# Second layer of a relational graph network: slot sums in three banks, placings three octets late, closes an octet later

## The chip, the cores and the metric

The kernel runs on one core of a Trainium2 chip. The metric is device time in microseconds for one execution. Five engines have programs of their own: PE (TensorE), DVE (VectorE), ACT (ScalarE), POOL (GpSimd) and SP (SyncE). They tell each other by semaphores what is done.

## The reference, cut to what matters

```python
def _rgcn_conv(x, src, dst, et, basis, comp, root, bias):
    W = jnp.einsum('rb,bio->rio', comp, basis)
    xw = jnp.einsum('ni,rio->nro', x, W)
    msgs = xw[src, et]
    seg = dst * N_REL + et
    summed = jax.ops.segment_sum(msgs, seg, num_segments=N_NODES * N_REL)
    cnt = jax.ops.segment_sum(jnp.ones((msgs.shape[0],), x.dtype), seg, num_segments=N_NODES * N_REL)
    mean = summed / jnp.maximum(cnt, 1.0)[:, None]
    agg = mean.reshape(N_NODES, N_REL, HIDDEN).sum(axis=1)
    return agg + x @ root + bias
...
h = x
for l in range(N_LAYERS):
    h_new = _rgcn_conv(h, src, dst, edge_type, basis[l], comp[l], root[l], bias[l])
    h_new = jax.nn.relu(h_new)
    h = h_new + h
...
x = _layernorm(x + h)
```

There are 12500 nodes, 200000 edges sorted by destination, 8 relations, 8 bases, 2 layers and 128 features, all in float32. The last line stands for the layernorm over the features of `x` plus the network's output.

## The kernel before

**Tiles and stages.** The edges are cut into 1563 tiles of 128, and 8 tiles make an octet, 196 octets in a layer (`NQ`). The nodes are cut into 98 blocks of 128 (`NT`). A layer goes through the octets in order. The first layer takes roughly the first 2320 us. It sums edges by node and relation, applies the relations' weights, and on the way stores the second layer's table `y_d` in memory: for each node and relation the message that an edge of that kind carries. The second layer, which the change concerns, gathers rows of `y_d` and sums them by destination.

**One octet of the second layer.** `FULL` = 192 of the 196 octets go this way (the last four go another, `add_rows`):

- POOL: `gather` issues eight indirect gathers (L677), each 128 rows of 512 bytes into a tile of `rows`. `rows` is a ring of seven octets. The gathers of octet n + 7 write the buffer of octet n, and so wait for the slot sum of n. From octet 190 on (`NQ - LATE`) gathers also wait for the last sum written by then, three octets back (`("done", 1)`).
- DVE: `slot_hots` makes eight matrices of 128x32 (L1090) that say for each edge of a tile which of 32 slots its destination has, times the edge's weight (one over the count), and, in the same step, the placing one-hot of 128x256 (L1093) that says for each slot where its node stands. It runs two octets ahead of the sums.
- PE: `slot_sums` (L1441), 8 matmuls, recorded as 16 instructions, sums the rows into the slots. Its output is one fixed PSUM bank, `misc`, the fourth quarter of `po1`.
- ACT: the copy (L627) takes the slots from that bank into a buffer `ys`, a ring of four.
- PE: `place_sums` (L1466), for the octet before, adds the copied slots to the accumulator of their block, `s0` or `s1` in turn. The first placing of a block (it *opens* the block) also adds the root term (L1470), from a copy of the block's old rows that ACT made (`open_block`, a ring of three: `id_k`, `id_r`, `jmp`).
- DVE: after a block's last placing `finish` closes it, in two steps. The first adds the carry from the block before (L1298) and takes out the next carry (L1302). The second, an octet later, is relu plus the old rows into `wide` (L1322).

A block takes the placings of two octets. After every eight blocks `norm` transposes `wide` on PE in two halves (L1573, also into `po1`) and DVE adds each half to `x` (L1581), one step of the list `todo` for each octet.

**What sets the order.** Each engine's program is written out by hand, in the order of the calls in the loop over `q` at the end of `ordered_path`. The class `Plan` derives the semaphore waits from what each step reads and writes: from named cells, of which every bank and every ring buffer is one. An engine signals where the program has a `plan.mark`. The gathers' order on POOL is set by `gathers(1, q)`, five octets ahead of the sums.

The output of a slot sum and the copy's ring, in code:

```python
b, bc = misc
m0 = b[:, 3, :]
...
o, oc = ys[q] = ys_r.take()
copy(o, m0, [bc], [oc])
```

## Time and profile before

| | us |
|---|---|
| median of three runs | 4590.76 (4581.87 to 4591.37) |
| profiled execution | 4590.46 |
| its span in the profile | 4588.4 |
| POOL busy, layer 2's gathers | 1475.1 |
| POOL idle just before them | 742.6 |
| PE busy on slot sums | 206.3 |
| DVE busy on slot one-hots | 352.8 |
| ACT busy on copies of the sums | 53.2 |

The span is the time between the first and the last event that the profiler recorded; 2.06 us of the execution lie around it. Busy times by engine and stretch follow, from the view of windows. The columns are the stretch in us, its length, then for each engine busy time and instructions, the mean granted TensorE clock, the DMA engines' busy share and GB/s. The first row is layer 1, the third nearly all of layer 2, the last its end.

```profile
0.00:2320.00 2320.00, 1424.22 (x7835) 1188.03 (x7836) 795.78 (x2491) 381.88 (x821) 1477.14 (x1571) 0.79 0.25 72
2320.00:2450.00 130.00, 31.73 (x178) 20.71 (x177) 20.38 (x66) 8.67 (x20) 70.90 (x77) 0.61 0.21 61
2450.00:4490.00 2040.00, 448.65 (x3492) 276.45 (x3490) 525.36 (x2178) 70.64 (x280) 1354.00 (x1435) 0.52 0.19 52
4490.00:4589.00 99.00, 36.87 (x250) 26.97 (x250) 43.38 (x156) 5.13 (x20) 51.30 (x55) 0.64 0.18 50
```

In the rows of groups and of the timeline that come later, `out<-in` are the program's names with the buffer numbers left out: `po` is the bank of the slot sums, `ys` the copied slots, `sT` the slot one-hots (they live in an old buffer of that name), `pl` and `iota_f` the placing one-hots, `s` a block's accumulator. What stands in brackets is the engine's idle time just before, and what ended it; "remote" means that the trace shows no local event that did. A row of waits has the line that waited, what released it, the total in us, the number of waits and the longest.

### The profile page before, as it was taken

What the parts mean: (1) busy time and instruction counts of PE and PEld (TensorE: products, weight loads), DVE (VectorE), ACT (ScalarE), POOL (GpSimd) and SP (SyncE); (2) the same over time, 40 slices, a digit from 0 to 9 for tenths busy, and PEclk for the clock granted to TensorE, in tenths of its full rate; (3) what the DMA queues carried; (4) which work ended last, traced back from release to release, by engine and by line L of the source; (5) the groups of instructions that cost most, each with busy time, mean ns of one, the idle gap of its engine ahead of it and who ended that gap; (6) DMA issues with size and microseconds to landing.
All of it is one profiled execution on the core that took longest, in us unless ns stands there. A gap on an engine that the chain in (4) does not pass through costs nothing.

```text
span 4588.4 us, 33820 instructions
## 1 busy us (share of the span) xinstructions
PE 1941.5 (42%) x11751; PEld 1512.2 (33%) x11751; DVE 1384.9 (30%) x4891; ACT 466.3 (10%) x1141; POOL 2953.3 (64%) x3135
## 2 busy tenths in 40 slices
PE   2666756666566666656731122222222222222213
PEld 1555555555455555545521111111111111111112
DVE  2544333333333323233321222222222222222224
ACT  0111112121111111111210000000000000000000
POOL 5666666666666666666556666666666666666665
PEclk9878778787777777777865555555555555555556
DMA  3111122232222222222221111212212212122121
GB/s 100 45 50 46 46 62 87 87 92 92 88 69 73 74 69 74 64 66 70 78 71 45 47 51 52 56 46 57 55 47 55 56 47 56 46 56 55 47 55 50
DMA packets 129812, 284.69 MB, mean 62 GB/s; under 512 B 54019, under 2 KB 61773, under 8 KB 129637
## 3 DMA queue, kind: packets, MB, share of 16 engines
q0 software_dynamic: 100064, 205.13, 17.2%
q10 hardware_dynamic: 16971, 52.05, 3.0%
q1 hardware_dynamic: 12602, 25.31, 1.6%
q8 instruction: 94, 1.54, 0.1%
q14 instruction: 81, 0.66, 0.0%
HBM read 223.63 MB, written 58.65 MB: 62 GB/s over the span
## 4 chain that ended last, share of the span: by engine, by line
another core or an unknown queue 64%; PE 20%; issue 8%; ACT 5%; DVE 2%; DMA 0%; POOL 0%; SPq 0%; ACTq 0%; POOLq 0%; DVEq 0%
PE y L1246 7%; PE s L1214 5%; ACT sT L627 2%; PE pt L1345 2%; PE po L1441 2%; ACT ys L627 1%; PE po L1277 1%; DVE dm L1121 1%; ACT y_row L627 1%; PE ct L1345 1%; PE ct L870 0%; PE po L1279 0%; PE ct L871 0%; PE pt L1183 0%
## 5 line engine op out<-in xcount | busy, mean ns | idle before, releaser
L677 POOL DMA_INDIRECT rows<-in_x_dram,idx x1563 | 1476.1, 944 | 841.7 <-issue 440.2
L677 POOL DMA_INDIRECT rows<-y_d,idy x1563 | 1475.1, 944 | 742.6 <-issue 453.3
L1441 PE MATMUL po<-rows,sT 128*32 128x128 f32 x3072 | 206.3, 411 | 1571.3 <-ACT ys L627 1151.2
L1246 PE MATMUL y<-w_sb,sT 128*128 128x128 f32 x3136 | 542.3, 345 | 526.2 <-ACT ys L627 198.6
L1246 PEld LDWEIGHTS y<-w_sb,sT 128*128 128x128 f32 x3136 | 509.4, 254 | 551.6 <-ACT ys L627 207.6
L1121 DVE TENSOR_SCALAR dm<-cols,kr,w 128x128 f32<-128x128 f16 x1563 | 526.2, 403 | 494.2 <-remote 203.1
L1441 PEld LDWEIGHTS po<-rows,sT 128*32 128x32 f32 x3072 | 121.9, 155 | 1658.1 <-ACT ys L627 1190.5
L1090 DVE TENSOR_SCALAR sT<-cols,kr,w 128x32 f32<-128x32 f16 x1536 | 352.8, 303 | 762.9 <-remote 617.7
L1214 PEld LDWEIGHTS s<-dm,rows 128*128 128x128 f32 x3126 | 436.3, 217 | 161.0 <-ACT sT L627 86.5
L1214 PE MATMUL s<-dm,rows 128*128 128x128 f32 x3126 | 450.5, 302 | 64.9 <-ACT sT L627 40.8
L627 ACT ACTIVATE sT<-s 128x512 f32<-128x512 f32 x391 | 212.5, 596 | 783.0 <-remote 556.8
L627 ACT ACTIVATE ys<-po 128x128 f32<-128x128 f32 x192 | 53.2, 277 | 2087.1 <-remote 1936.5
L1298 DVE TENSOR_TENSOR s<-s,carry 128x128 f32<-128x128 f32 x97 | 28.9, 298 | 670.8 <-remote 455.7
L1298 DVE TENSOR_TENSOR po<-po,carry 128x128 f32<-128x128 f32 x98 | 29.2, 298 | 655.1 <-remote 454.7
L1345 PE MATMUL pt<-w_sb,arena 128*128 128x512 f32 x258 | 157.3, 682 | 62.4 <-issue 50.0
L1466 PE MATMUL s<-pl,ys 128*128 128x256 f32 x288 | 167.9, 684 | 0.0
L1277 PE MATMUL po<-pl,ys 128*128 128x256 f32 x392 | 139.4, 440 | 24.2 <-issue 15.8
L627 ACT ACTIVATE y_row<-pt 128x512 f32<-128x512 f32 x131 | 78.4, 598 | 682.0 <-remote 484.2
L870 PE MATMUL ct<-arena,id_h 128*128 128x512 f16 (+1 forms) x188 | 75.5, 421 | 84.4 <-DVE arena L860 37.1
L860 DVE TENSOR_TENSOR arena<-cols,arena 128x129 f16<-128x129 f16 (+62 forms) x188 | 73.6, 408 | 69.5 <-remote 65.5
L1129 DVE TENSOR_SCALAR pl<-cols,pos 128x256 f32<-128x256 f16 x196 | 93.1, 476 | 0.0
L1466 PEld LDWEIGHTS s<-pl,ys 128*128 128x128 f32 x288 | 69.7, 301 | 53.3 <-issue 53.3
(212 smaller groups left out, 1409.7 us busy)
## 6 DMA issues: line engine op xcount, KB each, us to landing
y_d<-y_row ACTq DMA_DIRECT2D x96, 512.0 KB
rows<-in_x_dram,idx POOLq DMA_INDIRECT x1563
rows<-y_d,idy POOLq DMA_INDIRECT x1563
x_g<-in_x_dram SPq DMA_DIRECT2D x24, 512.0 KB
out_dram<-x_g SPq DMA_DIRECT2D x12, 512.0 KB
arena<-in_L_gnn_basis_dram SPq DMA_DIRECT2D x2, 512.0 KB
w_d<-y_row SPq DMA_DIRECT2D x2, 512.0 KB
w_sb<-w_d SPq DMA_DIRECT2D x2, 512.0 KB
```

Source lines behind the costliest of these rows:

```text
L627: act(lambda: nc.scalar.activation(out_t, in_t, AF.Copy), reads, writes)
L677: ins.append(nc.gpsimd.indirect_dma_start(out=t[:, i - q * Q, :], out_offset=None, in_=table_t, in_offset=bass.IndirectOffsetOnAxis(ap=ids ...
L870: nc.tensor.matmul(ct[:, :nb, :], id_h, eq[:, s - s0, :nb, main], start=(s == 1), stop=False)
L1090: vec(in_turn([lambda i=i: nc.vector.tensor_scalar(t[:, i, :], cols[:, :2 * K], kr[:, i0 + i:i0 + i + 1], w[:, i0 + i:i0 + i + 1], op0=ALU ...
L1121: emits.append(lambda i=i: nc.vector.tensor_scalar(t[:, i - q * Q, :wide], cols[:, :wide], ids[:, i:i + 1], w[:, i:i + 1], op0=ALU.is_equa ...
L1129: emits.append(lambda: nc.vector.tensor_scalar(o[:m], cols[:m], pos[:m, g // (2 * R), g % (2 * R):g % (2 * R) + 1], None, op0=ALU.is_equal))
L1214: last = nc.tensor.matmul(s_b[i // 4][0][:, i % 4, :], t[:, i, :], d[:, i, :], start=True, stop=True)
L1246: last = nc.tensor.matmul(y[:m], t[:, r, :nt, :].rearrange("p t k -> p (t k)"), w_sb[:, 0, r, :], start=(r == 0), stop=(r == R - 1))
L1277: ins = nc.tensor.matmul(a, o[:m], t[:m], start=opens, stop=last and not root_in)
L1345: pe(lambda: nc.tensor.matmul(hb[:n].rearrange("p r d -> p (r d)"), hT[:, j * P:j * P + n], w_sb[:, 1, k * H:(k + 1) * H, :].rearrange("p ...
L1441: last = nc.tensor.matmul(m0[i // 2 * 2 * K:(i // 2 + 1) * 2 * K, :], d[:, i, :], t[:, i, :], start=i % 2 == 0, stop=i % 2 == 1)
L1466: ins = nc.tensor.matmul(a, o[:m], t[:m], start=opens, stop=last and not root_in and not fixed)
```

## The change

All of it concerns layer 2; the instructions of layer 1 and POOL's order stay as they are.

- The slot sums use three banks in turn, the first quarters of `y`, `pt` and `ct`, which layer 1 used (`sum_b`).
- The copied slots go to a ring of six (`ys2_r`, in the old buffer `sT1`) in place of four.
- A placing comes three octets after its sum (`LAG`), not one.
- The placing one-hot has a step of its own, `slot_place`, an octet before it is used.
- A block's close starts one octet after its last placing, not in the same.
- The ring of blocks' old rows has four buffers, and each waits only for its own former user (`id_k`, `id_r`, `jmp` waited for all three).
- The norm's two halves use `po0` and `po1`, and each half's add is written one step after its transposes.
- At `q == FULL` the three placings that are left, and their closes, are written one after another.

Code lines move by 10 to 13: in the changed kernel the sums are L1451, placings L1478 and L1482, copies L628, placing one-hots L1097, closes L1307, L1311 and L1331.

```diff
+    LAG = 3
...
-        o, oc = pl[q] = pl2_r.take()
...
-            t[:, i, :], cols[:, :2 * K], kr[:, i0 + i:i0 + i + 1], w[:, i0 + i:i0 + i + 1], op0=ALU.is_equal,
-            op1=ALU.mult) for i in range(Q)]
-            + [lambda: nc.vector.tensor_scalar(o, cols, pos[:, q // (2 * R), q % (2 * R):q % (2 * R) + 1], None,
-                                               op0=ALU.is_equal)]),
-            ["cols", "rel", ("wt", q * Q // P), "pos"], new(c) + new(oc))
-        plan.mark("DVE")
+            op1=ALU.mult) for i in range(Q)]),
+            ["cols", "rel", ("wt", q * Q // P)], new(c))
+
+    def slot_place(q):
+        o, oc = pl[q] = pl2_r.take()
+        vec(lambda: nc.vector.tensor_scalar(o, cols, pos[:, q // (2 * R), q % (2 * R):q % (2 * R) + 1], None,
+                                            op0=ALU.is_equal),
+            ["cols", "pos"], new(oc))
 
     def onehot(l, q, g=None):
 
+        if l == 1:
+            for p in range(q - LAG, FULL if q == FULL + 1 else q - LAG + 1):
+                if 0 <= p < FULL and p not in pl:
+                    slot_place(p)
+            plan.mark("DVE")
         if l == 1 and q < FULL:
             slot_hots(q)
+            plan.mark("DVE")
...
-    old.update({("hb", i): ["id_k", "id_r", "jmp"] for i in range(3)})
+    old.update({("hb", i): [c] for i, c in enumerate(("id_k", "id_r", "jmp"))})
+    hb_b.append(home("sT1", P, "hb", 3))
+    ys2_r = Ring(None, [home("sT1", D, "ys2", i)[0] for i in range(6)], None, None, "ys2")
+    sum_b = [(b[:, 0, :], c) for b, c in (y_full, pt_b, ct_b)]
...
-        t, c = hb_b[k % 3]
+        t, c = hb_b[k % 4]
...
-        b, bc = misc
-        m0 = b[:, 3, :]
+        m0, bc = sum_b[q % 3]
...
-        o, oc = ys[q] = ys_r.take()
-        copy(o, m0, [bc], [oc])
+        o, oc = ys[q] = ys2_r.take()
+        copy(o, m0, [bc], new(oc))
...
-        for h, m in halves:
-            todo.append(lambda h=h, m=m: (turn(h, m), add(h, m)))
-        todo.extend([stats, aggr, root_of] + [lambda: None] * 5 + [one_by, scale, store])
+        todo.append(lambda: turn(*halves[0]))
+        todo.append(lambda: ([turn(*h) for h in halves[1:]], add(*halves[0])))
+        todo.append(lambda: ([add(*h) for h in halves[1:]], stats()))
+        todo.extend([aggr, root_of] + [lambda: None] * 5 + [one_by, scale, store])
...
+    def opening(p):
+        if 2 <= p < NQ and sup(p) != sup(p - 1):
+            open_block(sup(p))
+
+    def closed(j):
+        if j >= 0 and opened_by(j)[1]:
+            a, b = finish(1, sup(j))
+            a()
+            plan.mark("DVE")
+            ending.append((sup(j), b))
+
+    def ended():
+        for j, step in ending:
+            step()
+            plan.mark("DVE")
+            n = j // S
+            if j >= 0 and j % S == S - 1:
+                norm(n)
...
+        ending.clear()
...
-        late = q - 1
+        late = q - LAG
         if q < FULL:
             slot_sums(q)
-        if 0 <= late < FULL:
-            place_sums(late, sup(late), *opened_by(late))
+            if late >= 0:
+                place_sums(late, sup(late), *opened_by(late))
+        if q == FULL:
+            closed(late - 1)
+            for p in range(late, FULL):
+                place_sums(p, sup(p), *opened_by(p))
+                closed(p)
+                ended()
...
-        if sup(q + 2) != sup(q + 1) and q + 2 < NQ:
-            open_block(sup(q + 2))
+        if q < FULL - 1:
+            opening(late + 2)
+        elif q >= FULL:
+            opening(q + 2)
...
-                for j in [late] * (0 <= late < FULL) + [q] * (q >= FULL):
-                    if opened_by(j)[1]:
-                        a, b = finish(1, sup(j))
-                        a()
-                        ending.append((sup(j), b))
+                closed(q if near_end else late - 1)
```

How the instructions stand on the two engines that the change reorders follows, from the middle of layer 2. The first is PE before: sums into `po1`, from the ring `rows0` to `rows6`, with a placing of the octet before after each. Waits on `s_gq` are for gathers, on `s_DVE` for one-hots or closes, on `s_ACT` for copies.

```order
L1441 MATMUL po1_139<-rows2_106,sT0_112 32x128 [waits s_gq2,s_DVE,s_ACT]
L1441 MATMUL po1_139<-rows2_106,sT0_112 32x128 x7
L1466 MATMUL s1_136<-pl0_114,ys0_117 128x256
L1441 MATMUL po1_139<-rows3_107,sT0_112 32x128 [waits s_gq3,s_DVE,s_ACT]
L1441 MATMUL po1_139<-rows3_107,sT0_112 32x128 x7
L1466 MATMUL s0_135<-pl1_115,ys1_118 128x256 [waits s_DVE]
L1470 MATMUL s0_135<-id_r_124,w_sb_75 128x128
```

Now the same place in the changed kernel, with the copied sums in `sT1`:

```order
L1451 MATMUL pt_140<-rows5_109,sT0_112 32x128 [waits s_gq1,s_DVE,s_ACT]
L1451 MATMUL pt_140<-rows5_109,sT0_112 32x128 x7
L1478 MATMUL s0_135<-pl1_115,sT1_113 128x256 [waits s_DVE,s_ACT]
L1482 MATMUL s0_135<-jmp_81,w_sb_75 128x128
L1451 MATMUL ct_141<-rows6_110,sT0_112 32x128 [waits s_gq2]
L1451 MATMUL ct_141<-rows6_110,sT0_112 32x128 x7
L1478 MATMUL s0_135<-pl2_116,sT1_113 128x256
L1451 MATMUL y_137<-rows0_104,sT0_112 32x128 [waits s_gq3,s_DVE,s_ACT]
```

Every sum waited for ACT, that is for the copy just before it. Now every second one does, and the sum between them waits for its gathers alone. The banks differ from sum to sum, and a placing follows a sum that is three octets younger.

The second place is DVE before, two octets with a close (L1298, L1302, L1322):

```order
L1298 TENSOR_TENSOR s1_136<-s1_136,carry1_122 128x128 [waits s_PE]
L1302 TENSOR_SCALAR carry0_121<-s1_136,bias_t_76 128x128
L1090 TENSOR_SCALAR sT0_112<-cols_134,kr_71,w_72 128x32 x8
L1093 TENSOR_SCALAR pl0_114<-cols_134,pos_74 128x256
L1322 SCALAR_TENSOR_TENSOR wide1_131<-s1_136,id_r_124 128x128 [waits s_DVE]
L1090 TENSOR_SCALAR sT0_112<-cols_134,kr_71,w_72 128x32 [waits s_PE]
```

And in the changed kernel:

```order
L1097 TENSOR_SCALAR pl1_115<-cols_134,pos_74 128x256 [waits s_PE]
L1090 TENSOR_SCALAR sT0_112<-cols_134,kr_71,w_72 128x32 [waits s_PE]
L1090 TENSOR_SCALAR sT0_112<-cols_134,kr_71,w_72 128x32 x7
L1307 TENSOR_TENSOR s0_135<-s0_135,carry0_121 128x128 [waits s_PE]
L1311 TENSOR_SCALAR carry1_122<-s0_135,bias_t_76 128x128
L1097 TENSOR_SCALAR pl2_116<-cols_134,pos_74 128x256
L1090 TENSOR_SCALAR sT0_112<-cols_134,kr_71,w_72 128x32 [waits s_PE]
L1090 TENSOR_SCALAR sT0_112<-cols_134,kr_71,w_72 128x32 x7
L1331 SCALAR_TENSOR_TENSOR wide0_130<-s0_135,jmp_81 128x128 [waits s_DVE]
```

The number of instructions is the same. The placing one-hot now stands ahead of the slot one-hots and takes a wait on PE of its own in every second octet, and the slot one-hots between the close's two steps wait for PE too, which they did not before.

More of the change, by code (lines that the diff above doesn't have):

```diff
@@ L1453, in place_sums @@
         o, oc = ys.pop(q)
+        if opens:
+            acc[k] = acc_b[k % 2]
         a, ac = acc[k]
@@ L1566, in norm @@
         halves = [(h, min(4, k - 4 * h)) for h in range(-(-k // 4))]
-        b, bc = misc
         def turn(h, m):
+            b, bc = po_b[h]
             def emit():
@@ L1579, in add @@
         def add(h, m):
+            b, bc = po_b[h]
             zh = z[:, 4 * h:4 * h + m, :]
@@ L1849, in ordered_path @@
         opens, last = opened_by(q)
-        if opens:
+        if opens and q >= FULL:
             acc[k] = acc_b[k % 2]
@@ L1882, in ordered_path @@
         for i in range(2):
-            for j, step in ending:
-                step()
-                plan.mark("DVE")
-                n = j // S
-                if j >= 0 and j % S == S - 1:
-                    norm(n)
-                    if n + 2 < NX:
-                        todo.extend([lambda: None] * 2 + [lambda n=n: load_x(n + 2)])
-            ending.clear()
+            ended()
             if q == NQ - 2:
@@ L1897, in ordered_path @@
             elif i == 0:
-                for j in [late] * (0 <= late < FULL) + [q] * (q >= FULL):
-                    if opened_by(j)[1]:
-                        a, b = finish(1, sup(j))
-                        a()
-                        ending.append((sup(j), b))
+                closed(q if near_end else late - 1)
             if not near_end:
                 break
+        if q == FULL - 1:
+            for p in range(late + 2, FULL + 2):
+                opening(p)
         while near_end and todo:
```

3 lines of the change are left out of this document (2 added, 1 removed).

## The prediction

> **What bounds the kernel now.** I read the page's span, its busy times and its chain first.
>
> ```profile
> span 4588.4 us, 33820 instructions
> PE 1941.5 (42%) x11751; PEld 1512.2 (33%) x11751; DVE 1384.9 (30%) x4891; ACT 466.3 (10%) x1141; POOL 2953.3 (64%) x3135
> another core or an unknown queue 64%; PE 20%; issue 8%; ACT 5%; DVE 2%; DMA 0%; POOL 0%; SPq 0%; ACTq 0%; POOLq 0%; DVEq 0%
> L677 POOL DMA_INDIRECT rows<-y_d,idy x1563 | 1475.1, 944 | 742.6 <-issue 453.3
> L1441 PE MATMUL po<-rows,sT 128*32 128x128 f32 x3072 | 206.3, 411 | 1571.3 <-ACT ys L627 1151.2
> L627 ACT ACTIVATE ys<-po 128x128 f32<-128x128 f32 x192 | 53.2, 277 | 2087.1 <-remote 1936.5
> ```
>
> No engine is busy even two thirds of the span. The busiest is POOL, which issues the 1563 indirect gathers of each layer. Most of the chain (64%) is time with no visible owner. The change touches layer 2 alone, some 2320 to 4588 us, so I asked what POOL waits for there.
>
> ```profile
> POOL rows L677 <- issue: 457.4, 1492, 1.6
> POOL rows L677 <- remote: 280.5, 79, 8.6
> POOL jmp L673 <- DMA y_d<-y_row: 34.0, 1, 34.0
> POOL rows L677 <- PE po L1441: 11.2, 3, 10.6
> ```
>
> A gather takes 0.944 us and the pause before the next, when nothing holds it, 457.4 / 1492 = 0.307 us. POOL therefore needs 8 × (0.944 + 0.307) = 10.0 us per octet whatever the sums do. In 79 places it waits longer, 3.55 us on average, for something the trace only calls "remote". The timeline of a steady stretch shows what that is.
>
> ```profile
> 3053.36 1.11 PE L1441 MATMUL po<-rows,sT 128*32 128x128 f32 x16 [4.56 <-issue]
> 3054.40 1.22 PE L1466 MATMUL s<-pl,ys 128*128 128x256 f32 x2
> 3073.23 0.94 POOL L677 DMA_INDIRECT rows<-y_d,idy  x1 [0.30 <-issue]
> 3076.92 0.28 ACT L627 ACTIVATE ys<-po 128x128 f32<-128x128 f32 x1 [23.61 <-remote]
> 3077.15 0.94 POOL L677 DMA_INDIRECT rows<-y_d,idy  x1 [2.98 <-remote]
> 3077.25 1.10 PE L1441 MATMUL po<-rows,sT 128*32 128x128 f32 x16 [21.62 <-ACT ys L627]
> 3089.65 0.28 ACT L627 ACTIVATE ys<-po 128x128 f32<-128x128 f32 x1 [12.26 <-remote]
> 3089.89 0.94 POOL L677 DMA_INDIRECT rows<-y_d,idy  x1 [3.06 <-remote]
> 3089.98 1.10 PE L1441 MATMUL po<-rows,sT 128*32 128x128 f32 x16 [10.05 <-ACT ys L627]
> ```
>
> The 16 instructions of a slot sum start at 3053.36 and by their records end at 3054.47. The copy out of their bank starts at 3076.92, 22.4 us later, and POOL goes on 0.23 us after the copy: it waits for the same sum, whose ring buffer the next gathers overwrite. The next sum starts 0.33 us after the copy, because it writes the same bank, and the next copy comes 11.6 us after that sum's recorded end. So a finished sum becomes known to the other engines late, by anything from 0.1 to 24 us. I call this the **lag**. With one bank the lags stand in a row, one per octet.
>
> By the Trainium skill (Perfetto Trace Analysis, "Tensor Engine Instruction (MATMUL, LD_WEIGHTS)") a matmul's end in a profile is computed from its size, and the semaphore goes out only when PSUM has acknowledged the writes. Taken with these rows it allows a lag that the records don't show; it gives no size for one. If the recorded ends were the real ones, by the rows an octet's chain would be 1.11 + 0.28 + 0.33 = 1.7 us, never a bound, and the change would be worth nothing; the 22.4 us between recorded end and copy speak against that.
>
> ```profile
> 2447.24 0.28 ACT L627 ACTIVATE ys<-po 128x128 f32<-128x128 f32 x1 [49.23 <-remote]
> 4508.19 0.28 ACT L627 ACTIVATE ys<-po 128x128 f32<-128x128 f32 x1 [13.17 <-remote]
> ```
>
> These are the copies of the sums of octets 2 and 183: 181 octets in 2060.95 us, 11.39 us each. POOL alone would need 10.0. The serial lag costs about 1.4 us per octet, and that is all the change can win.
>
> **The change part by part.** The profiled run took 4590.46 us (span 4588.4, 2.06 around it), practically the median of the three runs shown, 4590.76. I make the sum against 4590.5.
>
> **Three banks** (the order's rows show y, pt and ct taking turns). A sum no longer waits for the copy of the sum before it, but of the third before. Lags of three sums run side by side, and POOL may run on. POOL's idle time in the layer is 742.6 us; 1563 pauses of 0.307 are 479.2 of it, and 742.6 − 479.2 = 263.4 us is the wait on late sums. Some of it stays:
>
> ```profile
> 4515.28 0.94 POOL L677 DMA_INDIRECT rows<-y_d,idy  x1 [10.62 <-PE po L1441]
> 4549.38 0.94 POOL L677 DMA_INDIRECT rows<-y_d,idy  x1 [4.21 <-remote]
> 4571.92 0.94 POOL L677 DMA_INDIRECT rows<-y_d,idy  x1 [0.30 <-issue]
> ```
>
> The last gathers wait for a sum three octets back rather than seven, which is not changed: 10.62 + 4.21 − 2 × 0.30 = 14.2 us stay. Removable: 263.4 − 14.2 = 249.2 us.
>
> How much of that comes back is the one large unknown, since no row shows three sums in flight. Bounds: at best nothing comes back, 4590.5 − 249.2 = 4341. At worst each group of three (191 / 3, about 63) still costs POOL one wait of the present mean, 3.55 − 0.30 = 3.25, so 205 us come back: 4546. Between them I ask how often three sums together exceed what POOL gives them. POOL spends 30 us on three octets and may be seven ahead. The longest steady lag that I quote, 22.4 us, plus the slot one-hots that the next sum may wait for (1.84 us, below) and the group's own 1.1 makes 25.3, or 8.4 us per octet: under 10.0. Only several long lags in a row use up the lead, while today one does. That is nearer the lower end; I take an eighth of the 205, **26 us**.
>
> **Placing three octets later, its one-hots separate, the ring of copied sums longer (4 to 6).** Every matmul, copy and one-hot is still issued, once each; nothing is added. Placing now reads a sum whose copy is long done, and the one-hot that waits for an old placing no longer stands in one group with the slot one-hots.
>
> ```profile
> 3089.71 1.84 DVE L1090 TENSOR_SCALAR sT<-cols,kr,w 128x32 f32<-128x32 f16 x8 [8.35 <-remote]
> 3091.47 0.47 DVE L1093 TENSOR_SCALAR pl<-cols,pos 128x256 f32<-128x256 f16 x1
> 3078.34 0.30 DVE L1298 TENSOR_TENSOR s<-s,carry 128x128 f32<-128x128 f32 x1 [21.63 <-PE po L1441]
> 3078.55 0.34 DVE L1302 TENSOR_SCALAR carry<-s,bias_t 128x128 f32<-128x128 f32 x1
> 3081.07 0.29 DVE L1322 SCALAR_TENSOR_TENSOR wide<-s,id_k 128x128 f32<-128x128 f32 x1
> ```
>
> VectorE spends 1.84 + 0.47 per octet and 0.93 per close, one close in two octets: 2.8 us of every 10. PE spends 1.11 + 1.22 and, every second octet, 0.64: 2.7 us. Both are covered by POOL's issuing, so I count 0. At the end of the layer three placings and their closes run in a row: about 3 × 1.22 + 2 × 0.93, 5.5 us, under the 22.5 us of issuing from 4549.38 to the last gather. 0, or 5.5 if that cover were gone.
>
> **Closing an octet later.** This can cost. While VectorE waits in a close, the slot one-hots for later sums are behind it; and the block after next can't be opened before the close is through. Today's waits there:
>
> ```profile
> ACT ys L627 <- remote: 1832.9, 126, 25.1
> DVE s L1298 <- remote: 447.8, 47, 22.4
> PE po L1441 <- ACT ys L627: 1120.1, 75, 23.0
> ```
>
> They already happen at every second close without being on POOL's path. An octet's delay lets the placing's lag (9.5 us on average, 447.8 / 47) pass before VectorE arrives. Bounds: a gain of nothing (POOL is not faster than 10.0), a loss of the fourth case below. I take 0.
>
> **A fourth buffer for a block's old rows, each buffer waiting only for its own predecessor.** The first opening copy need no longer wait for the one repair gather:
>
> ```profile
> 2374.34 0.94 POOL L673 DMA_INDIRECT jmp<-y_d,fix_i  x1 [34.02 <-DMA y_d<-y_row]
> 2386.98 0.31 ACT L627 ACTIVATE id_k<-arena 128x128 f32<-128x128 f32 x1 [16.72 <-DMA rows<-y_d,idy]
> ```
>
> The copy of sum 0 stood behind it on ACT; PE gets up to 9 us back there. POOL has its ring of seven free at that point and does not gain: 0. Its own 34.0 us wait stays.
>
> **The norm's halves in two banks, added a step later.** Same transposes, same adds. They stop sharing a bank with the sums, which is part of the 263.4 already counted: 0 on top. Two adds of 0.69 (row below) for each 1024 of the 12500 nodes are 17 us, the most it could cost if they stood on POOL's path; I keep 0.
>
> ```profile
> 4562.59 0.69 DVE L1581 TENSOR_TENSOR x_g<-po,x_g 128x512 f32<-128x512 f32 x1 [1.21 <-PE po L1573]
> ```
>
> Sum: 4590.5 − 249.2 + 26 = **4367 us**.
>
> **The rivals.**
>
> *The lag grows when POOL stops idling.* In the rows above both late copies, at 3076.92 and 3089.65, come a few us after POOL ran dry, as if results got through mainly then. At the layer's start, with seven octets free to issue, the copy at 2447.24 came 49.23 us after ACT went idle, and 3.0 us after POOL's last free gather (2444.24, the row that ended that run). Then three banks only give POOL a longer run before the same pause: the worst case above, 4590.5 − 263.4 + 14.2 + 205 = 4546. Against it: the copy at 3053.03, and others, came while POOL was issuing, and a pause that releases one sum today would release three.
>
> ```profile
> 2444.24 0.94 POOL L677 DMA_INDIRECT rows<-y_d,idy  x1 [0.30 <-issue]
> 3053.03 0.28 ACT L627 ACTIVATE ys<-po 128x128 f32<-128x128 f32 x1 [6.50 <-remote]
> ```
>
> *The change doesn't do what it says.* A semaphore wait written in by the planner could still order the sums one after another. The order shows a wait on ACT at every second sum, though, for a copy some three octets old. Then the time stays at 4590.
>
> *Slower: the two blocks' banks become the loop.* A block's bank is opened again only after its last placing is visible (one lag), the close has run an octet later behind slot one-hots that wait for a sum (a second lag), and the second step (L1322) is done; PE's program has all later sums behind that opening. Round trip: two lags and, from rows, about 13 us of work and octet order (two slot sums 2.2, three placings with a root 4.3, two sets of one-hots 4.6, a close 0.9, a copy and hand-overs 1.2), per four octets. With the means of today, 1832.9 / 126 = 14.5 and 9.5, that is (24 + 13) / 4 = 9.3 us per octet, just under POOL's 10.0. It decides from a mean of some 13.5 us per lag up. At 18 each it is 49 / 4 = 12.3 us per octet, 0.9 more than today's 11.39: 181 × 0.9 = 163 us, 4750.
>
> **How the numbers follow.** Lags shared, POOL nearly free: 0.60, with a range of its own from 4318 (the whole 263.4 gone and a measurement 9 us low) to 4440 (some 100 us come back, half of the 205). Lag grows: 0.19, about 4546. No effect: 0.05, 4590. Block loop: 0.16, about 4750. The predicted time is the first, 4367. The range takes in the first two and the no-effect case, 4318 to 4595, about 8 in 10 after what lies outside the first case's own range. About 0.2% (9 us) is what a measurement here can tell from no change. Faster by more: 0.60 + 0.19 = 0.79; the same: 0.05; slower: 0.16.
>
> **What would show it.** Right: POOL's "remote" wait in layer 2 falls from 280 to some 40 us; the sums are no longer released by the copy (1120.1 us now); copy to copy takes 10.0 to 10.3 us; the span ends near 4365. Wrong: "remote" stays above 200 with longer single waits (lag grows), the sums' wait on the copy stays (no effect), or PE waits for VectorE's second step at the opening placings (block loop). A different time in layer 1, whose order is the same, would be none of these.

## The result and the profile after

The change made no difference that can be measured: 4592.82 us (median of 12 runs, 4570.81 to 4598.6) against 4590.87 before (12 runs, 4573.55 to 4595.11), a ratio of 1.0004 with an interval of 0.9993 to 1.0015. The forecast was 4367. The time lies within the stated range of 4318 to 4595 only because that range took in the no-effect case.

The page of the changed kernel, its span, busy times, chain and the group of layer 2's gathers:

```profile
span 4591.8 us, 33830 instructions
PE 2244.1 (49%) x11751; PEld 1595.3 (35%) x11751; DVE 1379.6 (30%) x4892; ACT 464.7 (10%) x1141; POOL 2953.9 (64%) x3135
another core or an unknown queue 31%; issue 24%; PE 23%; POOL 12%; DVE 6%; ACT 4%; DMA 1%; SPq 0%; POOLq 0%; ACTq 0%; DVEq 0%
L678 POOL DMA_INDIRECT rows<-y_d,idy x1563 | 1475.0, 944 | 742.6 <-issue 459.6
```

POOL's idle time ahead of layer 2's gathers is 742.6 us, to the tenth what it was. PE looks busier by 303 us with as many instructions, and the chain's share without an owner went from 64% to 31%, with "issue" at 24%. The view of waits says who is waiting now, for POOL and for PE:

```profile
POOL rows L678 <- issue: 464.3, 1512, 1.8
POOL rows L678 <- remote: 165.2, 44, 10.6
POOL rows L678 <- PE s L1482: 47.7, 10, 5.8
...
POOL rows L678 <- PE y L1451: 22.8, 4, 5.7
POOL rows L678 <- PE s L1478: 20.7, 4, 5.7
POOL rows L678 <- PE pt L1451: 20.1, 3, 8.7
POOL rows L678 <- PE ct L1451: 9.9, 2, 5.6
...
PE ct L1451 <- issue: 368.7, 301, 3.1
PE y L1451 <- issue: 360.7, 284, 6.3
PE pt L1451 <- issue: 319.5, 240, 3.8
...
PE s L1478 <- DVE wide L1331: 68.5, 35, 20.9
```

The sums' wait for the copy (1120.1 us before) is gone, as forecast. In its place stands "issue": PE waits for nothing that the profile shows, in over 800 places, between matmuls of one sum. POOL's waits for results are fewer and longer, the six rows without the pauses (the row left out is the repair gather's): 286.4 us in 67 waits. Before they were 280.5 + 11.2 = 291.7 us in 82. The timeline shows what that looks like (start, duration, engine, and in brackets the idle time before):

```profile
3033.93 0.66 PE L1451 MATMUL ct<-rows,sT 128*32 128x128 f32 x16
...
3058.78 0.94 POOL L678 DMA_INDIRECT rows<-y_d,idy  x1 [0.30 <-issue]
3059.70 0.37 PE L1451 MATMUL pt<-rows,sT 128*32 128x128 f32 x1 [2.21 <-issue]
3061.10 0.37 PE L1451 MATMUL pt<-rows,sT 128*32 128x128 f32 x1 [1.03 <-issue]
3062.50 0.37 PE L1451 MATMUL pt<-rows,sT 128*32 128x128 f32 x1 [1.03 <-issue]
3063.20 0.42 PE L1451 MATMUL pt<-rows,sT 128*32 128x128 f32 x1 [0.33 <-issue]
3063.90 1.16 PE L1451 MATMUL pt<-rows,sT 128*32 128x128 f32 x12 [0.28 <-issue]
3063.96 0.28 ACT L628 ACTIVATE sT<-ct 128x128 f32<-128x128 f32 x1 [25.77 <-remote]
3064.20 0.94 POOL L678 DMA_INDIRECT rows<-y_d,idy  x1 [4.47 <-remote]
3068.22 1.10 PE L1451 MATMUL ct<-rows,sT 128*32 128x128 f32 x16
```

Single matmuls of one sum start 0.70 or 1.40 us apart, though nothing lies between them in the program. POOL has run dry at 3059.72; 4.2 us later PE does the rest of the sum, 12 instructions in 1.16 us, and what was outstanding becomes known to ACT and POOL. A few us later a sum of 16 again takes 1.10. PE's own starts are **held up**, then, and it goes on in bursts. That comes beside the late news and not in its place: the sum in `ct` that ACT copies at 3063.96 has all its 16 records by 3034.59, 29.4 us before. Over the whole layer, 174 of the 192 copies start more than 2 us after the recorded end of their sum, 16.0 us on average (before: 135, 9.3 us), and in 105 sums the starts are spread over more than 1.2 us (before: none). Whether PE stands still or only its signals back up, these records, whose ends are computed, can't tell.

Octets 70 to 186 of the changed kernel take 11.35 us each, the difference of the first gathers of the two divided by 116:

```profile
3139.50 0.94 POOL L678 DMA_INDIRECT rows<-y_d,idy  x1 [0.30 <-issue]
4456.24 0.94 POOL L678 DMA_INDIRECT rows<-y_d,idy  x1 [0.30 <-issue]
```

The same two gathers before the change start at 3145.25 and 4460.20, 11.34 us an octet (the prediction's 11.39 goes from copy to copy, over octets 2 to 183). Everything about the sums was rearranged, and the pace did not move.

### The profile page after: what moved, and what is told of

The parts are those of the page before. It is cut to its first block, busy times and chain, and to the rows that moved or that the text cites. A ratio compares the mean times of both kernels' runs of the same rounds, so it can differ in the third digit from the quotient of the medians.

```text
span 4591.8 us, 33830 instructions
## 1 busy us (share of the span) xinstructions
PE 2244.1 (49%) x11751; PEld 1595.3 (35%) x11751; DVE 1379.6 (30%) x4892; ACT 464.7 (10%) x1141; POOL 2953.9 (64%) x3135
## 4 chain that ended last, share of the span: by engine, by line
another core or an unknown queue 31%; issue 24%; PE 23%; POOL 12%; DVE 6%; ACT 4%; DMA 1%; SPq 0%; POOLq 0%; ACTq 0%; DVEq 0%
POOL rows L678 12%; PE y L1255 7%; PE s L1223 5%; DVE sT L1090 3%; ACT sT L628 2%; PE pt L1354 2%; PE s L1478 2%; PE po L1286 1%; DVE dm L1130 1%; PE y L1451 1%; PE ct L1451 1%; PE ct L1354 1%; PE pt L1451 1%; ACT y_row L628 1%
## 5 line engine op out<-in xcount | busy, mean ns | idle before, releaser
L678 POOL DMA_INDIRECT rows<-y_d,idy x1563 | 1475.0, 944 | 742.6 <-issue 459.6
L1451 PE MATMUL ct<-rows,sT 128*32 128x128 f32 x1024 | 177.1, 385 | 391.1 <-issue 368.7
L1451 PE MATMUL y<-rows,sT 128*32 128x128 f32 x1024 | 170.3, 392 | 382.1 <-issue 360.7
L1451 PE MATMUL pt<-rows,sT 128*32 128x128 f32 x1024 | 152.7, 389 | 343.7 <-issue 319.5
L628 ACT ACTIVATE sT<-s 128x512 f32<-128x512 f32 x391 | 212.5, 596 | 785.9 <-remote 542.1
L1451 PEld LDWEIGHTS ct<-rows,sT 128*32 128x32 f32 x1024 | 73.5, 141 | 484.2 <-issue 470.3
L1451 PEld LDWEIGHTS y<-rows,sT 128*32 128x32 f32 x1024 | 71.7, 145 | 473.6 <-issue 466.8
L1478 PE MATMUL s<-pl,sT 128*128 128x256 f32 x288 | 165.2, 641 | 140.1 <-issue 95.6
L1307 DVE TENSOR_TENSOR po<-po,carry 128x128 f32<-128x128 f32 x98 | 29.1, 297 | 640.9 <-remote 448.5
L1451 PEld LDWEIGHTS pt<-rows,sT 128*32 128x32 f32 x1024 | 67.5, 144 | 422.9 <-issue 413.9
L628 ACT ACTIVATE y_row<-pt 128x512 f32<-128x512 f32 x131 | 78.4, 598 | 689.5 <-remote 516.6
L1478 PEld LDWEIGHTS s<-pl,sT 128*128 128x128 f32 x288 | 72.0, 286 | 208.1 <-issue 205.6
```

The costliest lines, as they stand in the source:

```text
L628: act(lambda: nc.scalar.activation(out_t, in_t, AF.Copy), reads, writes)
L678: ins.append(nc.gpsimd.indirect_dma_start(out=t[:, i - q * Q, :], out_offset=None, in_=table_t, in_offset=bass.IndirectOffsetOnAxis(ap=ids ...
L1307: emits.append(lambda: nc.vector.tensor_add(a[:, :n], a[:, :n], t[:, :n]))
L1451: last = nc.tensor.matmul(m0[i // 2 * 2 * K:(i // 2 + 1) * 2 * K, :], d[:, i, :], t[:, i, :], start=i % 2 == 0, stop=i % 2 == 1)
L1478: ins = nc.tensor.matmul(a, o[:m], t[:m], start=opens, stop=last and not root_in and not fixed)
```

## The experiments

Each is one run with a profile, beside one run of the kernel before on the same chip. The runs came on three chips. On two of them the kernel before takes 4592 to 4620 us, on the third 3934.54, which turned out to matter. The 12 runs of one kernel above spread over 22 and 28 us, and a difference of that size between two single runs says nothing.

**Is it PE's work?** The slot sums halved, narrowed, doubled:

```diff
-            for i in range(Q):
+            for i in range(0, Q, 2):        # e1, start and stop at each
+                ... [:, :64] of both        # e2
+            for i in [*range(Q)] * 2:       # e3
```

> Changed kernel with four of a slot sum's eight matmuls left out (every second tile's edges don't count in layer 2). Theory 1, TensorE itself gets through its instructions slowly in layer 2, whatever bank they write: an octet has 11 instructions on PE in place of 19, so PE needs 11.4 x 11/19 = 6.6 us an octet, under POOL's 10.0, and the time falls to 4340 to 4390. Theory 2, only the news of a finished sum is late, a lag for each sum: nothing changes, 4582 to 4600. Theory 3, the two accumulators' close and reopening is the loop: nothing changes either.

> Changed kernel with the slot sums' matmuls half as wide (64 of 128 features are summed in layer 2), as many instructions. Theory 1 with a price for each instruction: 4582 to 4600. Theory 1 with a price by the data that a matmul moves: 4340 to 4450. Theories 2 and 3: 4582 to 4600.

> Changed kernel with every slot sum's matmuls issued twice (the second pass starts the sum anew, so the output is the same). Theory 1: 35 instructions an octet in place of 19, at 0.6 us each 9.6 us more per octet, 192 octets, 6400; if only part of them is slow, at least 5000. Theory 2: 1.1 us more per sum where PE has 7 us to spare, 4585 to 4620. Theory 3: the same as theory 2.

4571.13, 4596.75 and 4618.4 us, beside 4595.1. Theory 1, a TensorE that is slow by itself, is refuted at both ends: half the matmuls saved 24 us and not 200, twice as many cost 23 and not over 400. (The 4571.13 is also 11 us under the range of theories 2 and 3, within the spread.) PE does more of them in each burst; one of e3:

```profile
3073.57 2.39 PE L1451 MATMUL pt<-rows,sT 128*32 128x128 f32 x30
```

Theories 2 and 3 stood.

**Is it POOL?** Plain loads of as many bytes from SP's queue in place of the gathers:

```diff
+        elif l == 1 and SOON // Q < q < NQ - LATE:
+            r0 = q % 90 * Q * P
+            load(t, y_d[r0:r0 + Q * P, :].rearrange("(p i) d -> p i d", i=Q), reads, [cell + (0,), cell + (1,)])
```

> Changed kernel with the indirect gathers of octets 3 to 189 of layer 2 replaced by one plain load of as many bytes each from SP's queue (other rows of the table are summed), so that POOL is silent there. Theory 1 with POOL's issuing as what slows TensorE: an octet takes its work alone, some 3 us, so layer 2 takes 600 to 900 us and the whole 2950 to 3300. Theory 1 with a TensorE that is slow by itself: 11.4 us an octet remains, 4450 to 4600. Theory 2: the lag of one sum in three remains, 3 to 8 us an octet, 3000 to 3900. Theory 3 with its two lags: about the same.

2983.73 us. The stretch of plain loads, in the columns of the view of windows:

```profile
2420.00:2880.00 460.00, 308.29 (x3195) 198.95 (x3194) 459.65 (x1991) 66.00 (x257) 0.00 (x0) 0.77 0.61 208
```

VectorE works all the time, and an octet takes 2.80 us (from copy to copy, octets 10 to 180). By its time alone the run is only 16 us under the range of theory 2, 3000 to 3900; the copies decide. They start 0.10 us (median) after the recorded end of their sum, so no lag is left. Theory 2 (a lag of its own for each sum) falls, and theory 3 too: the two accumulators are in the same loop here. What holds PE up comes with the gathers, be it POOL's issuing or what follows it.

From here there were two theories. **H**: gathers advance at some 1.42 us each, whoever waits; POOL issues at 1.25, gets ahead, and PE is held up until the rest has caught up. **S**: PE is held up whenever POOL issues. First by a drain after each gather, alone and with a memset:

```diff
+                    if l == 1:
+                        nc.gpsimd.drain()
+                        nc.gpsimd.memset(pace, 0.0)     # e6 only
```

> Changed kernel with a drain on POOL after every gather of layer 2, which adds a little to each gather's 1.25 us (how much, the profile will show; call it d). Theory H, a server behind POOL takes about 1.42 us for a gather (POOL's 1475 us busy and 743 idle over 1563 gathers), POOL runs ahead of it at 1.25, and TensorE gets little done until it has caught up: the time stays 4580 to 4610 up to d = 0.17, POOL's waits for PE shrink by what the drains cost, and the matmuls' steps of 0.70 us become rarer. Theory S, TensorE is held up whenever POOL issues, at whatever pace: POOL's waits for PE stay near 280 us and the time grows by 1563 x d, 4670 for d = 0.05, 4750 for 0.10.

> The same with a drain and a memset of one column after every gather, so a larger d. Theory H: up to d = 0.17 no change, 4580 to 4610; beyond, POOL never waits for PE and the time is 2320 + 1563 x (1.25 + d) + 100. Theory S: as much more as the run before by its d.

7533.47 and 7573.54 us, beside 4620.2. Both expectations were for a small d. A gather of e5 takes 3.31 us, so d is 2.06. With it theory S gives 4620 + 1563 x 2.06 = 7840, theory H 4620 + 1563 x (2.06 - 0.17) = 7574. The time is nearer H, but POOL stands still for over 2 of the 3.3 us, and an S that holds only while POOL issues isn't excluded. The timeline of e5 shows that at 3.3 us a gather sums are prompt:

```profile
4021.27 1.11 PE L1453 MATMUL ct<-rows,sT 128*32 128x128 f32 x16 [24.39 <-DMA rows<-y_d,idy]
4022.45 0.28 ACT L628 ACTIVATE sT<-ct 128x128 f32<-128x128 f32 x1 [26.35 <-PE ct L1453]
```

PE waits for the gathered rows, does its 16 at once, and ACT copies 0.07 us after the recorded end. Next, on the same chip, gathers of half the rows and of half the bytes:

```diff
-                        out=t[:, i - q * Q, :], ...  ap=ids[:, i:i + 1]
+                        out=t[:64, i - q * Q, :], ...  ap=ids[:64, i:i + 1]              # e7
+                        out=t[:, i - q * Q, :64], in_=table_t.rearrange("n (h d) -> (n h) d", h=2)   # e8
```

> Changed kernel with 64 rows in place of 128 in every gather of layer 2 (the other half of each tile is stale, so its edges count wrongly). If POOL's instruction costs by its rows, 0.94 us becomes about 0.5, and the theories differ in what is left: H with a server that costs by rows, an octet at half of 11.4 us, 3450 to 3700; H with a server that costs by instruction, 4500 to 4600; S, POOL's own 8 x 0.8 = 6.4 us and the same pauses, 3850 to 4050.

> Changed kernel with gathers of 256 bytes a row in place of 512 in layer 2 (half of each row is stale). If what holds TensorE or POOL is the data that moves into the tiles: 4340 to 4450. If it goes by rows or instructions (theory H by rows, and theory S): 4575 to 4600.

4634.78 and 4627.23, beside 4620.2: neither rows nor bytes. The assumption in the first, that POOL's instruction would cost half, was wrong. The gathers' group of e7, then of e8:

```profile
L678 POOL DMA_INDIRECT rows<-y_d,idy x1563 | 1412.1, 903 | 829.5 <-issue 467.8
L678 POOL DMA_INDIRECT rows<-y_d,idy x1563 | 1475.0, 944 | 761.5 <-issue 452.7
```

On the same chip POOL spends 63 us less on issuing in e7 and idles 68 us longer. Busy and idle together are 2241.6 and 2236.5 us. POOL's own time for a gather is not what counts. One thing these two runs did not halve: the DMA packets (the pieces in which the gathers' bytes move). Their queue has as many as in the changed kernel, whose row comes first, then that of e7; only the MB, in the second place, are fewer.

```profile
q0 software_dynamic: 100064, 205.13, 17.1%
q0 software_dynamic: 100064, 153.91, 13.3%
```

That is 32 packets for each of 3127 gathers (both layers' and the repair gather).

The next four ran on the third chip, where the kernel before takes 3934.54 us. Waits long satisfied as a pace, drains at some octets, and one bank again:

```diff
+                        for _ in range(4):                              # e9, 12 in the other
+                            nc.gpsimd.wait_ge(plan.sems["PE"], 1)
+                if l == 1 and (10 <= q < 70 or 70 <= q < 130 and q % 2 == 0 or 130 <= q < 186 and q % 4 == 0):
+                    nc.gpsimd.drain()                                   # e10
-        m0, bc = sum_b[q % 3]
+        m0, bc = sum_b[0]                                               # e11
```

> Changed kernel with four waits on a value long reached after each gather of layer 2 from octet 3 on: POOL works through a few more instructions, each perhaps 0.02 to 0.06 us, so d is 0.08 to 0.25 us a gather (the profile will show it). Theory H: up to d = 0.17 the time stays within 15 us of the kernel before and POOL's waits for PE shrink by what d adds. Theory S: the waits stay and 1530 x d is added, 120 to 380 us.

> The same with twelve such waits, d three times as long. Theory H: once 1.25 + d is over 1.42, POOL never waits for PE, sums are copied within a few us of their start, and the time is that of the kernel before plus 1530 x (d - 0.17). Theory S: plus 1530 x d.

> Changed kernel with a drain on POOL after every octet of gathers for octets 10 to 69, after every second for 70 to 129 and after every fourth for 130 to 185. The idle time at a drain is 2.3 us after a single gather. Theory H, POOL runs ahead of a server by 0.17 us a gather: idle at a drain 2.3 + 8 x 0.17 = 3.7, 2.3 + 16 x 0.17 = 5.0 and 2.3 + 32 x 0.17 = 7.7 us. Theory S: 2.3 us at each, since nothing piles up. A pile that is bounded would show as a value that stops growing.

> Changed kernel with all slot sums in one bank again (y), all else as changed. Theories H and S: within 15 us of the kernel before, with the matmuls recorded in one piece of 1.1 us and the copies late, as before the change. If the banks did bring something that the late placing or the closes took back, the time is over 4620.

3936.43, 3929.71, 4201.99 and 3927.78 us. The waits added nothing to a gather (no row of the case had priced one; the 0.02 to 0.06 us of the expectation was a guess), so e9 is no test of pace; but on this chip there is nothing to test. The gathers' groups of e11, one bank:

```profile
L678 POOL DMA_INDIRECT rows<-in_x_dram,idx x1563 | 1477.5, 945 | 480.2 <-issue 471.5 <-DMA arena<-in_dst_dram 4.2 <-PE ct L1354 0.9
L678 POOL DMA_INDIRECT rows<-y_d,idy x1563 | 1476.8, 945 | 476.3 <-issue 476.3
```

POOL never waits for a sum, with one bank as with three, and 10.0 us an octet is its own issuing. Layer 1 is shorter too: its idle time is 480 us in place of 842. The same instructions of POOL take the same 0.94 us on both kinds of chip; only the hold-up is missing. This chip was used once, for these four runs and the kernel before, so whether the difference stays with the chip isn't shown.

A real pace needs work on POOL: memsets, each waiting for the one before. With them the drains and the single bank ran again, this time on a chip where the kernel before takes 4592.39:

```diff
+                    for _ in range(1 * (l == 1 and q > SOON // Q)):   # 3 in e13
+                        if paced:
+                            nc.gpsimd.wait_ge(pace_sem, len(paced))
+                        nc.gpsimd.memset(pace, 0.0).then_inc(pace_sem, 1)
+                        paced.append(q)
```

> Changed kernel with one memset of 128x48 on POOL after each gather of layer 2 from octet 3 on, each waiting for the memset before; it adds d to a gather's 1.25 us, by the profile, perhaps 0.1 to 0.2. On a chip where the kernel before takes about 4600, theory H: for d up to 0.17 the time stays within 15 us of the kernel before and POOL's waits for PE shrink by 1530 x d; theory S: the waits stay near 280 us and the time grows by 1530 x d. On a chip where it takes about 3935: plus 1530 x d by both.

> The same with three such memsets, d about three times as large, 0.3 to 0.6. On a chip of about 4600, theory H: sums are copied within a few us of their start, POOL waits for no sum any more, and the time is that of the kernel before plus 1530 x (d - 0.17); theory S: late sums and POOL's waits stay, plus 1530 x d. On a chip of about 3935: plus 1530 x d.

> The run with few drains again (after every octet, every second, every fourth). On the chip of 3935 us its idle times at a drain were 2.68, 3.03 and 3.66 us for 8, 16 and 32 gathers, 0.04 us more for each gather. On a chip of about 4600, theory H: 3.7, 5.0 and 7.7 us or a bound below it; theory S: the same values as on the other chip.

> The run with one bank again. On a chip of about 4600, theories H and S: within 15 us of the kernel before, the matmuls recorded in one piece of 1.1 us and the copies late. If the three banks bring something that the late placings take back: over 4620.

4598.91, 5030.25, 4668.83 and 4584.7 us. One memset adds only 0.02 us (two gathers of a run of them start at 3052.02 and 3053.29, 1.27 apart), and POOL's whole time stays: 1488.2 + 422.4 for gathers, 240.5 + 77.4 for memsets, 2228 us where the changed kernel has 2218. With so small a d the two theories differ by 31 us (1530 x 0.02), too little for a single run.

```profile
L680 POOL DMA_INDIRECT rows<-y_d,idy x1563 | 1488.2, 952 | 422.4 <-issue 249.8 <-remote 120.9 <-PE pt L1458 13.7
L686 POOL MEMSET pace<- 128x48 f32 x1539 | 240.5, 156 | 77.4 <-remote 61.9 <-issue 11.6 <-POOL pace L686 3.2
```

Three memsets make a gather 1.71 us (octets 10 and 186, below: 2410.30 us for 176 octets, 13.70 each), and there theory H held and S fell: with d = 0.46, H gives 4592 + 1530 x (0.46 - 0.17) = 5036 us and S 5296; POOL's waits for sums are gone, and a copy follows its sum at once, on a chip with the hold-up. First the two gathers, then one sum and its copy, then POOL's only wait for a result in the layer, all of e13:

```profile
2480.07 0.95 POOL L680 DMA_INDIRECT rows<-y_d,idy  x1 [0.56 <-issue]
4890.37 0.95 POOL L680 DMA_INDIRECT rows<-y_d,idy  x1 [0.56 <-issue]
...
3042.42 1.10 PE L1458 MATMUL ct<-rows,sT 128*32 128x128 f32 x16 [11.44 <-DMA rows<-y_d,idy]
3043.60 0.28 ACT L630 ACTIVATE sT<-ct 128x128 f32<-128x128 f32 x1 [13.40 <-PE ct L1458]
...
POOL rows L680 <- remote: 3.3, 1, 3.3
```

The drains bracket the limit more closely. The first gathers of octets 10, 70, 130 and 186, on the third chip (e10) and then on this one (e10b):

```profile
2062.33 0.94 POOL L678 DMA_INDIRECT rows<-y_d,idy  x1 [0.30 <-issue]
2806.73 0.94 POOL L678 DMA_INDIRECT rows<-y_d,idy  x1 [2.89 <-issue]
3488.04 0.94 POOL L678 DMA_INDIRECT rows<-y_d,idy  x1 [0.30 <-issue]
4094.37 0.94 POOL L678 DMA_INDIRECT rows<-y_d,idy  x1 [0.30 <-issue]
```

```profile
2465.58 0.94 POOL L678 DMA_INDIRECT rows<-y_d,idy  x1 [10.57 <-remote]
3210.57 0.94 POOL L678 DMA_INDIRECT rows<-y_d,idy  x1 [2.65 <-issue]
3891.78 0.95 POOL L678 DMA_INDIRECT rows<-y_d,idy  x1 [0.30 <-issue]
4533.01 0.94 POOL L678 DMA_INDIRECT rows<-y_d,idy  x1 [0.30 <-issue]
```

| us per octet | chip of 3934 | chip of 4592 | copy after the octet's last gather there, mean |
|---|---|---|---|
| drain at every octet | 12.41 | 12.42 | 3.1 |
| every second | 11.36 | 11.35 | 5.9 |
| every fourth | 10.83 | 11.45 | 48.8 |
| changed kernel, no drain | | 11.35 | 62 |

(The copy's delay is its start less the end of the octet's last gather, over the octets of that third. On the chip of 3934 it is 2.9 us in all three. The 62 is of the changed kernel's own profile; before the change it was 64.) Down to 11.35 us an octet POOL sets the pace and sums are prompt on either chip. Where POOL could do 10.83, the chip with the hold-up still takes 11.4, and its sums go late until POOL has to wait. The part of H that placed the limit in POOL itself did not hold: the idle time at a drain was 2.7, 3.0 and 3.7 us after 8, 16 and 32 gathers (medians) on both chips alike, not the 3.7, 5.0 and 7.7 expected of a pile there. And one bank, e11b, is again within 8 us of the kernel before. Its page of waits has the old shape, ACT's copies waiting 1866.5 us on "remote" and POOL 273.5:

```profile
POOL rows L678 <- remote: 273.5, 61, 11.5
```

The last two, on a chip of 4614.38, ask whether the limit goes by gathers or by what they read:

```diff
-                        in_offset=bass.IndirectOffsetOnAxis(ap=ids[:, i:i + 1], axis=0)))
+                        ... ap=ids[:, q * Q - q * Q % P:q * Q - q * Q % P + 1]             # e14, octets 3 to 189
-            plan.add("POOL", some(i0, i0 + n), reads, ...
+            plan.add("POOL", some(i0, i0 + n // 2), reads, ..., n=n // 2)                  # e15, octets 3 to 189
```

> Changed kernel in which the gathers of octets 3 to 189 of layer 2 use one column of indices for 16 octets, so that they read the same 128 rows of the table again and again (the sums are of other rows). On a chip of about 4600: if the limit of 1.42 us a gather lies in reading scattered rows of the memory, an octet takes 10.0 us and the time falls to 4340 to 4400; if it goes by the instruction, 4580 to 4630. On a chip of about 3935: no change.

> Changed kernel with four gathers an octet in place of eight in octets 3 to 189 of layer 2 (the other four tiles are stale, so their edges count wrongly), PE, DVE and ACT as before. On a chip of about 4600: a limit by gather instruction gives 4 x 1.42 = 5.7 us an octet with late sums, 4595 - 187 x 5.67 = 3535, and within 40 of it; if what sets the pace is the octet (a sum's news, a wait per octet), it stays near 4600; if POOL alone sets it at 5.0 us, 3410. On a chip of about 3935: 3935 - 187 x 5.0 = 3000.

4621.24 and 3591.53 us. Reading the same rows changes nothing. Half the gathers save 1023 us, 5.47 for each of the 187 octets; sums are still late. Busy and idle time of POOL for 815 gathers:

```profile
L678 POOL DMA_INDIRECT rows<-y_d,idy x815 | 770.9, 946 | 426.8 <-issue 228.2 <-remote 112.3 <-PE s L1484 21.4
```

That is 1197.7 / 815 = 1.47 us each, beside 2217.6 / 1563 = 1.42. The limit goes nearly by the gather. Of the 56.5 us over the expectation (3591.5, not 3535) 19.4 come from the kernel before, which takes 4614.4 here and not 4595; the other 37.1 are 0.2 us an octet that it leaves open. POOL's own 5.0 an octet (3410) and a pace by the octet (4600) are refuted. So is a weaker S, by which PE catches up in POOL's pauses: these pauses would have to go by PE's work, of which e1 and e3 halved and doubled the sums and e15 left all as it was.

## Why the prediction was wrong

- **What bounds the kernel** was read one step short. The rows were right: POOL waits for late sums, 263.4 us. The step that failed is "The serial lag costs about 1.4 us per octet, and that is all the change can win". It took the lag as a delay of a sum, given from outside, and the 11.39 us as the sum of such delays. The runs show the reverse: the pace of 11.35 to 11.4 us is given (1.42 us a gather on these chips), and the lag is what fills the difference. With one bank it stands between a sum and its copy, with three it is spread over three sums; that longer buffers would only take in more of it is to be expected, but wasn't run.
- **"Removable: 249.2 us"** was therefore removable by none of the edits. POOL's wait changed its shape (67 waits, not 82) and not its size, 286.4 us after 291.7. The rows put only 165.2 of it to "remote", so the stated sign "stays above 200" was not met to the letter; the rest, 121.2 us, stands under PE's lines. Copy to copy, forecast at 10.0 to 10.3 us, stayed at the old pace.
- **The put-back, taken as 26 us**, was all of the 249.2. Its bounds were reasoned from the lags of today, as if these stayed when POOL runs faster. The rival "the lag grows when POOL stops idling" (0.19) had the right sign: the copies came 16.0 us after the recorded ends, not 9.3. Its price, one wait of today's mean for each group of three, has the same fault: the waits grew.
- **"No effect"** (0.05) gave the time, 4590, for a reason that is not the case: the sums do overlap; PE has up to three outstanding. That the time lies in the stated range is therefore luck.
- **The block loop** (0.16) did not decide. PE waited for the close's second step at an opening in 35 places, 68.5 us in all: that sign of the rival did show, but the pace of 11.35 us stayed, and with one bank (e11b) too. Its lag of 14.5 us was also read too high: 1832.9 / 126 is how long ACT stood idle before a copy, and from recorded end to copy it was 9.3 on average.
- **One reading was off.** The copy at 3089.65 comes 11.3 us after the recorded end of its sum (3077.25 + 1.10), not 11.6; nothing in the sum rests on it.
- **The covers** held: placing later, the closes, the separate one-hots, the flush at the end and the norm's two banks cost nothing visible. The one-bank runs, 4584.7 on one chip and 3927.78 on the other (8 and 7 us under the kernel before, single runs, within their spread), say the same of everything but the banks.
- **A sign was in the profile before.** Layer 1's gathers took 1476.1 + 841.7 = 2317.8 us, 1.48 each; layer 2's 1475.1 + 742.6 = 2217.7, 1.42 each. The two layers give PE quite different work and wait for different sums. That two such stages come out at almost the same price per gather, well over the 1.25 that POOL needs, speaks for a limit on gathers and against a lag of layer 2's sums. The late copy at the layer's start, 49 us with seven octets free to issue, and the bursts after POOL's pauses, both quoted in the prediction, pointed there too. The row of layer 1:

```profile
L677 POOL DMA_INDIRECT rows<-in_x_dram,idx x1563 | 1476.1, 944 | 841.7 <-issue 440.2
```

The Trainium skill's remark that a matmul's recorded end is computed (Perfetto Trace Analysis, "Tensor Engine Instruction (MATMUL, LD_WEIGHTS)") led the same way as the rows, and these runs bound it: where PE is not held up, the copy starts 0.07 to 0.08 us after the recorded end (e5, e13), so the estimate is good there. Where it is, the one-bank kernels record 16 starts within 1.1 us and a copy up to 25 us later.

What stays open: what the limit is. It goes by gathers, not by their rows, bytes or addresses, not by PE's instructions. Whether it goes by the instruction or by its 32 packets isn't told apart, since e15 halved both. It is absent on one of the three chips; POOL's drains don't see it, and PE and POOL's own memset signals (e12, 61.9 us "remote") feel it. No faster version came out of the runs; a correct kernel with fewer gathers wasn't tried.

One rival is untested, and the traces point to it. A trace also keeps records of the semaphore updates that tell of a DMA's landing. Over octets 10 to 185 there are 16 of them per gather on the chip without the hold-up (16.1 to 16.3 in e9, e10 and e11, a few other DMAs counted in), and POOL's waits have no "remote" there. In the kernel before, the changed one, e7, e8, e11b, e12 and e14 there are only 2.6 to 3.2. In the three thirds of e10b it is 12.4, 6.2 and 2.8, in e13 about 14.7, in e5 16.2. The later the sums, the more records are missing, so the hold-up may lie on the way by which such signals or their records travel. All times here are of executions that the profiler recorded. Whether recording takes part in the limit, or the loss is another effect of it, no run decides.

## What to carry to other kernels

Where a wait on a result grows and shrinks with what hides it, divide the whole time of the stage by the units of the engine that waits. If two stages with different work give the same price per unit, suspect that the lag is backlog behind a limit on that unit; more buffers then only move it, as here. The cheap test is to slow that engine slightly, or to double the suspected work: if the time stays, the wait was not what cost it. And look at the same kernel on another chip before trusting a hold-up to be the program's, and at whether the trace has all its records before reading what a "remote" wait waits for.

## What the hardware did that was not expected

- In the changed kernel TensorE advances in steps of 0.70 us (0.7, 1.4, 2.1, 2.8 between single matmuls) while gathers are issued back to back. It goes in full bursts from about 4 to 6 us after POOL stops (most of the 50 places where POOL waited over 2 us) until some 6 to 10 us after it resumes.
- Chips differ: the same kernel takes 3934.54 us on one and 4592 to 4620 on two others, nearly all of it POOL's waits in both layers. Between the profile before and that of e11 (one bank, on the faster chip), 663 us apart, POOL's idle time before gathers differs by 361.5 us in layer 1 and 266.3 in layer 2, and its wait for the last store of `y_d` by 33.7.
- Of the records of landings, 16 per gather where nothing is held up (e11), only 3 are left where it is (the kernel before).
- A gather of 64 rows costs POOL 0.903 us, one of 128 rows 0.944; half the bytes changed nothing (0.944).
- The idle time at a drain on POOL is 2.3 to 2.4 us after one gather, 3.7 after 32 back to back. Up to twelve waits on a value long reached cost POOL nothing between two gathers (1.25 us as without).
